# Two stacked graph-attention layers on one core: SyncE transfers in written order, other places for layer 0 steps at the seams, other row-sum chains

## The chip, the cores and the metric

The kernel runs on one core of a Trainium2 chip. The time is the device time of one execution in microseconds; of the kernel before there are three runs, with a median of 4371.78 us (4368.92 to 4374.29). Everything else is read from one profiled execution.

## The reference

Eight samples of 2048 nodes with 256 features; one adjacency matrix for all. Two layers, each with a residual and a layer norm:

```python
# layer 0, 8 heads of 32 features
x_proj = einsum('bnd,hdf->bhnf', x, W)
e = leaky_relu(e_src[..., :, None] + e_dst[..., None, :], 0.2) + softplus(beta) * log(adj + 1e-6)
attn = softmax(where(adj > 0, e, -inf), axis=-1)
x1 = layernorm(x + (attn @ x_proj) @ W_out.T)
# layer 1, one head of 256
e = leaky_relu((x1 @ W1) @ (x1 @ W2).T, 0.2)
attn = softmax(where(adj > 0, e, -1e12), axis=-1)
out = layernorm(x1 + relu(attn @ (x1 @ W3)))
```

## The kernel before

Node tiles have 128 rows, so a sample has 16. All arithmetic is in float32.

**Layer 0** (class `Gat`) of one sample takes 64 steps, called units here: four passes `hp` of two heads, each over 16 key tiles `jt`. A unit loads one row block of the transposed mask m^T (`mt`, 128x2048, 1 MB; line 200, two buffers), lets VectorE form the unnormalised attention of each head over all 2048 queries in one instruction (`s`, line 342, from the query factors `c`, the key factors `re` and `mt`; four buffers, so two units), and lets TensorE add its product with the projected values `v` into `val` and with the key factors into the row sums `den` (both line 367). For some key tiles, listed in `SUMMED` (line 67), `den` is left out: a chain of tiles is added up in `d`, the first tile by ScalarE (line 355), the others by VectorE (line 349, issued one unit later), and one product with ones at the end of the pass puts the chain into `den`. At the end of a pass `finish` (line 371) copies `val` into `ht` and `den` into `dn`, spreads the four rows of `dn` over the partitions (`rc`, line 385), takes the reciprocal (386), stores it (387), and after every second pass loads it broadcast (`rb`, 393) and multiplies `ht` (395).

**Between the layers**, `output` (line 397) forms x1 in four groups of four tiles: product y with W_out (420), residual, layer norm, store. `turn` (line 436) transposes x1 and forms h3 = x1 W3, two tiles at a time.

**Layer 1** (class `Dot`) takes 16 steps, one for each query tile. A step transposes the first quarter of the weights p of its tile (line 500), forms the scores e of the next tile (481), adds the mask `pen` and takes the minimum of the negative on VectorE (486), exponentiates on ScalarE (487), transposes the rest and accumulates p h3 in `acc` (516). Then it scales, loads its x1 row (521), adds it (524), normalises and stores.

**Order.** TensorE's order is the written one (`manual_schedule`, line 86). Everything else, SyncE's transfers among it, is ordered by the framework's planner, which takes the instructions by their place in the program and by when it expects them ready. Every engine works through its own list in order; SyncE issues all loads and most stores and waits at a transfer until its buffer is free.

The program first builds m^T, runs layer 0 of sample 0 and projects all other samples; v and the factors `re` of samples 2 to 7 are stored in DRAM. Then the main loop (line 595) works on layer 1 of sample b-1 and layer 0 of sample b together: `layer_0(n)` places n units, and `dot.step` takes a function that is called at three places of a step: ahead of it, after the next tile's scores (before the accumulation), and after the accumulation. At the hand-over, the seam, steps 14 and 15 of the sample before are still to be done; then come the x1 groups, `turn`, and the first query tile of the next sample. Units 0 and 1 follow step 14's accumulation, then come step 15, two x1 groups, units 2 and 3, two groups, units 4 and 5, and units 6 to 11 between the pieces of `turn`. `fresh.load()` (line 603) loads v, for which there is one buffer, and `re`, for which there are three. The tag `ht` of `chunk` has three buffers, shared by `dn`, the x groups and the query projections h1.

## Time and profile before

| | before |
|---|---|
| median of 3 runs | 4371.78 us |
| profiled execution | 4370.06 us, its span 4368.3 us |
| granted TensorE clock | 0.989 |
| TensorE busy | 4226.0 us, 97% |
| VectorE busy | 3618.2 us, 83% |
| ScalarE busy | 1669.7 us, 38% |
| m^T loads | 496 of 1024 KB, 4.9 us to landing |
| period of one sample (2 to 7) | 506 us |

The span is the time from the first to the last instruction of the profiled execution. In a group of instructions, the line reads: line of the code, engine, operation, output<-inputs, shapes and count | busy time in us, mean ns of one | idle time of the engine just before them, and what ended it. In an engine's list in order of time, the first number is the start in us, the second the length of the stretch; a bracket gives the idle time before it and what ended it. Matmuls overlap, so TensorE's lengths overlap as well.

### The profile page before, as it was taken

How to read it: one execution, taken by the hardware profiler on the slowest of the kernel's cores; microseconds unless marked ns; L12 is line 12 of the kernel's file. 1: busy time of each engine (PE TensorE's matmuls, PEld its weight loads, DVE VectorE, ACT ScalarE, POOL GpSimd, SP SyncE). 2: the span in 40 equal slices, each digit the busy share in tenths (PEclk: the TensorE clock that was granted, in tenths of full speed). 3: DMA queues.
4: the chain of work that ended last, by engine and by line, in shares of the span. 5: the costliest groups of instructions: out<-in, count | busy, mean ns of one | idle time of the engine just before them, and what ended most of it. 6: DMA issues, size and time to landing. Idle time of an engine off the chain costs nothing.

```text
span 4368.3 us, 59747 instructions
## 1 busy us (share of the span) xinstructions
PE 4226.0 (97%) x25008; PEld 2221.4 (51%) x25008; DVE 3618.2 (83%) x2598; ACT 1669.7 (38%) x3021; POOL 9.5 (0%) x14
## 2 busy tenths in 40 slices
PE   7999899999999999999999999999999999999999
PEld 4444344455455554445545554455455554555666
DVE  6888888998889898998889988898999988898222
ACT  6522233333333433333333334333333333333454
POOL 0000000000000000000000000000000000000000
PEclk9999899999999999999999999999999999999999
DMA  8877666656555654556555565555545565554211
GB/s 252 297 267 281 230 214 215 228 195 226 186 189 189 215 194 156 201 185 220 178 193 193 177 212 183 190 193 208 184 171 193 193 221 179 188 184 141 72 50 41
DMA packets 250959, 839.10 MB, mean 192 GB/s; under 512 B 32320, under 2 KB 150848, under 8 KB 175424
## 3 DMA queue, kind: packets, MB, share of 16 engines
q1 hardware_dynamic: 215360, 801.71, 52.6%
q10 hardware_dynamic: 35328, 33.56, 2.2%
q8 instruction: 196, 3.21, 0.3%
q14 instruction: 75, 0.61, 0.0%
HBM read 761.53 MB, written 73.14 MB: 191 GB/s over the span
## 4 chain that ended last, share of the span: by engine, by line
PE 64%; DVE 16%; issue 7%; DMA 2%; ACT 2%; SPq 0%; ACTq 0%; DVEq 0%; POOLq 0%
PE acc L516 18%; PE e L481 16%; PE val L367 13%; DVE s L342 10%; PE den L367 9%; PE pt L500 5%; DVE d L349 4%; DMA mt<-mt_d 2%; PE h1p L471 1%; PE y L420 1%; PE proj L268 1%; DVE st L424 1%; DVE ht L422 1%; PE h3p L451 1%; DVE p L486 0%
## 5 line engine op out<-in xcount | busy, mean ns | idle before, releaser
L342 DVE SCALAR_TENSOR_TENSOR s<-c,re,mt 128x2048 f32<-128x2048 f32 x1024 | 2351.1, 2342 | 179.2 <-PE den L367 113.8
L367 PE MATMUL val<-s,v 128*32 128x512 f32 x8192 | 1031.4, 604 | 69.3 <-DVE s L342 69.2
L516 PE MATMUL acc<-h,pts 128*128 128x256 f32 x4096 | 951.0, 380 | 4.3 <-ACT pts L502 4.0
L481 PE MATMUL e<-x1t,h 128*128 128x512 f32 x2048 | 906.3, 595 | 6.5 <-ACT h L473 6.5
L516 PEld LDWEIGHTS acc<-h,pts 128*128 128x128 f32 x4096 | 749.3, 190 | 94.5 <-ACT pts L502 8.3
L367 PE MATMUL den<-s,re 128*32 128x512 f32 x5568 | 702.2, 596 | 3.2 <-ACT dn L382 3.2
L349 DVE SCALAR_TENSOR_TENSOR d<-s,re,d 128x2048 f32<-128x2048 f32 x272 | 631.4, 2343 | 0.1
L481 PEld LDWEIGHTS e<-x1t,h 128*128 128x128 f32 x2048 | 379.1, 190 | 459.4 <-issue 416.7
L367 PEld LDWEIGHTS val<-s,v 128*32 128x32 f32 x8192 | 245.9, 110 | 692.7 <-issue 513.9
L502 ACT COPY pts<-pt 128x512 f32<-128x512 f32 x512 | 298.3, 583 | 738.0 <-PE pt L500 731.7
L483 ACT ACTIVATE p<-e 128x512 f32<-128x512 f32 x512 | 302.9, 595 | 433.6 <-PE e L481 430.1
L486 DVE CUSTOM_DVE_ANT_0 p<-p,pen 128x2048 f32<-128x2048 f32 x128 | 292.9, 2289 | 210.9 <-ACT p L483 210.3
L367 PEld LDWEIGHTS den<-s,re 128*32 128x32 f32 x5568 | 193.0, 111 | 426.1 <-issue 412.4
L500 PEld LDWEIGHTS pt<-ident,p 128*128 128x128 f32 x2048 | 240.1, 141 | 227.8 <-issue 156.1
L487 ACT ACTIVATE p<-p,neg 128x2048 f32<-128x2048 f32 x128 | 256.6, 2005 | 224.0 <-DVE neg L486 224.0
L500 PE MATMUL pt<-ident,p 128*128 128x128 f32 x2048 | 318.6, 279 | 14.4 <-ACT p L487 14.4
L524 DVE TENSOR_TENSOR z<-z,x1r 128x256 f32<-128x256 f32 x128 | 53.8, 421 | 178.7 <-ACT z L523 175.3
L523 ACT ACTIVATE z<-acc,rec 128x256 f32<-128x256 f32 x128 | 60.6, 474 | 365.5 <-PE acc L516 332.8
L268 PE MATMUL proj<-wp,xt 128*128 128x272 f32 (+1 forms) x512 | 132.3, 402 | 11.6 <-ACT both L272 8.5
L451 PE MATMUL h3p<-w3s,x1t 128*128 128x256 f32 x512 | 120.8, 381 | 2.6 <-ACT x1t L446 2.6
L355 ACT ACTIVATE d<-s,re 128x2048 f32<-128x2048 f32 x56 | 111.9, 2002 | 23.0 <-DMA xg<-in_x_dram 16.1
L268 PEld LDWEIGHTS proj<-wp,xt 128*128 128x128 f32 x512 | 93.3, 192 | 51.4 <-issue 21.0
(89 smaller groups left out, 1886.0 us busy)
## 6 DMA issues: line engine op xcount, KB each, us to landing
mt<-mt_d SPq DMA_DIRECT2D x496, 1024.0 KB, 4.9
c<-c_d SPq DMA_DIRECT2D x64, 1024.0 KB, 6.3
pen<-pen_d SPq DMA_DIRECT2D x112, 512.0 KB, 3.4
xg<-in_x_dram SPq DMA_DIRECT2D x60, 512.0 KB, 5.7
adj_t<-in_adj_dram SPq DMA_DIRECT2D x16, 1024.0 KB, 8.0
mt_d<-mt SPq DMA_DIRECT2D x16, 1024.0 KB, 5.6
rb<-rec_d SPq DMA_DIRECT2D x64, 256.0 KB, 4.4
x_d<-ht ACTq DMA_DIRECT2D x32, 512.0 KB, 3.9
```

What stands on the lines that cost most here:

```text
L268: nc.tensor.matmul(t[:, 0:cols], xt[:, kc, ts(it % IG, P)], wp[:, kc, 0:cols], start=(kc == 0), stop=(kc == KC - 1))
L342: nc.vector.scalar_tensor_tensor(sa, self.cs[a], self.re[:, 0, jt, h:h + 1], mt, ALU.max, ALU.mult)
L349: nc.vector.scalar_tensor_tensor(d, sa, e[:, jt - 1, h:h + 1], d, ALU.mult, ALU.add)
L367: nc.tensor.matmul(dst[ts(q, DH), ts(c, BK)], weights[q % 2], s[q % 2][:, ds(q // 2 * HALF + c * BK, BK)], start=start, stop=stop)
L451: nc.tensor.matmul(t[:, ts(i, D)], x1t[:, kc, ts(2 * (j - 1) + i, P)], w3s[:, kc, :], start=(kc == 0), stop=(kc == KC - 1))
L481: nc.tensor.matmul(t, self.h1[:, kc, ts(it % IG, P)], self.x1t[:, kc, ts(c, BK)], start=(kc == 0), stop=(kc == KC - 1))
L483: nc.scalar.activation(p[:, ts(c, BK)], t, AF.Prelu, alpha=ALPHA)
L486: nc.vector.tensor_tensor_reduce(p, p, pen, -1.0, FMAX, ALU.add, ALU.min, neg)
L487: nc.scalar.activation(p, p, AF.Exp, bias=neg, scale=-1.0, accum_out=den)
L500: nc.tensor.transpose(t[:, ts(k, P)], p[:, ts(g * IG + k, P)], ident)
L502: nc.scalar.copy(pt, t)
L516: nc.tensor.matmul(acc, now[:, ts(k, P)], self.h3[:, j, :], start=(j == 0), stop=(j == NT - 1))
```

## The change

From the main loop on, SyncE's order is the written one too. m^T loads are placed two units ahead of their use and c loads as soon as a buffer is released in the written order (`load_ahead`, `follow`). `finish` becomes a generator that a pass's next units carry on, one part a unit (`later`): after its copies, the loads of `rc` with the reciprocal are placed two units later, the store one unit after that, and rb one more. rb takes two half tiles from the tag `ht` instead of one whole tile of the chain's tag `d`. pen_d is stored after its first use. The chains have three key tiles (2, 4, 5) in pass 0, and in the others five tiles for sample 1 and seven for samples 2 to 7. At the seam, x1 groups, `turn` and pairs of units alternate, three x groups are loaded ahead, and 20 units are placed before the regular steps, where there were 16.

```diff
@@ -64,7 +64,9 @@
     NP = H // HP
     IG = BK // P
-    SUMMED = [(), (1, 3, 6, 9, 12)] + [(1, 3, 6, 8, 11, 13)] * (B - 2)
+    SUMMED = [[()] * NP, [(2, 4, 5)] + [(1, 4, 7, 10, 13)] * (NP - 1)]
+    SUMMED += [[(2, 4, 5)] + [(1, 3, 5, 7, 9, 11, 13)] * (NP - 1)] * (B - 2)
     const = ctx.enter_context(tc.tile_pool(name="const", bufs=1))
     dram = ctx.enter_context(tc.tile_pool(name="dram", bufs=1, space=DRAM))
@@ -210,7 +212,6 @@
             a = chunk.tile([P, HALF], I32, tag="ht", name="adj_r", bufs=3)
             nc.sync.dma_start(a, adj[ts(it, P), ts(s, HALF)])
             nc.vector.tensor_scalar(pen[:, ts(s, HALF)], a, 0.0, NO_EDGE, ALU.is_le, ALU.mult)
-        nc.sync.dma_start(pen_d[ts(it, P), :], pen)
         return pen
     def layer_norm(z):
@@ -237,6 +238,7 @@
             self.b = b
             self.units = ((hp, jt) for hp in range(NP) for jt in range(NT))
             self.ms, self.mts = [], []
+            self.later = gats[b - 1].later if b > 1 else []
         def begin(self, kept):
@@ -315,6 +317,21 @@
             nc.sync.dma_start(c, c_d[self.b, h:h + 1, :].to_broadcast([P, N]))
             return c
+        def load_ahead(self):
+            self.mt_loads = (load_mt(jt, False) for _ in range(self.b, B) for _ in range(NP) for jt in range(NT))
+            self.c_loads = (gats[b].query_rows(h) for b in range(self.b, B) for h in range(H))
+            self.mts, self.cs_ahead = [], []
+            for _ in range(2):
+                self.cs_ahead.append(next(self.c_loads))
+                self.mts.append(next(self.mt_loads))
+            self.cs_ahead.append(next(self.c_loads))
+        def follow(self, gat):
+            self.mt_loads, self.c_loads, self.mts, self.cs_ahead = gat.mt_loads, gat.c_loads, gat.mts, gat.cs_ahead
         def more_mt(self, count, ahead=0):
             while len(self.mts) < min(count, NT):
@@ -327,23 +344,36 @@
             for _ in range(count):
                 hp, jt = next(self.units)
+                for work in list(self.later):
+                    if next(work, self) is self:
+                        self.later.remove(work)
                 if jt == 0:
-                    self.cs = [self.query_rows(hp * HP + a) for a in range(HP)]
+                    if self.b > 0:
+                        self.cs = [self.cs_ahead.pop(0) for _ in range(HP)]
+                    else:
+                        self.cs = [self.query_rows(hp * HP + a) for a in range(HP)]
                     self.val = pacc.tile([P, HALF], F32, tag="val", name="val")
                     self.den = pacc.tile([P, HALF], F32, tag="den", name="den")
                 first = self.b == 0 and hp == 0
                 if first:
                     self.more_mt(jt + 2, jt > 0)
-                mt = self.mts[jt] if first else load_mt(jt, self.b == 0)
+                if self.b > 0:
+                    mt = self.mts.pop(0)
+                else:
+                    mt = self.mts[jt] if first else load_mt(jt, True)
                 s = []
                 for a in range(HP):
                     h = hp * HP + a
                     sa = wide_tile("s", "s", 4)
                     nc.vector.scalar_tensor_tensor(sa, self.cs[a], self.re[:, 0, jt, h:h + 1], mt, ALU.max, ALU.mult)
                     s.append(sa)
+                    if self.b > 0 and jt == NT - 1:
+                        self.cs_ahead += [c for c in [next(self.c_loads, None)] if c]
+                if self.b > 0:
+                    self.mts += [t for t in [next(self.mt_loads, None)] if t]
                 v, e = self.v, self.re[:, 1]
                 heads = [hp * HP + a for a in range(HP)]
-                chain = SUMMED[self.b]
+                chain = SUMMED[self.b][hp]
                 if jt - 1 in chain[1:]:
                     for d, sa, h in zip(self.sums, self.last, heads):
                         nc.vector.scalar_tensor_tensor(d, sa, e[:, jt - 1, h:h + 1], d, ALU.mult, ALU.add)
@@ -359,7 +389,13 @@
                 if chain and jt == NT - 1:
                     self.products(self.den, [ones] * HP, self.sums, False, True)
                 if jt == NT - 1:
-                    self.finish(hp)
+                    work = self.finish(hp)
+                    next(work)
+                    if self.b == 0:
+                        for _ in work:
+                            pass
+                    else:
+                        self.later.append(work)
         def products(self, dst, weights, s, start, stop):
             for c in range(HALF // BK):
@@ -380,19 +417,24 @@
                                self.val[ts(s, HP * DH), :].rearrange("p (t i) -> p t i", i=P))
             dn = chunk.tile([P, HALF], F32, tag="ht", name="dn", bufs=3)
             nc.scalar.copy(dn, self.den)
+            yield
+            yield
             rc = small.tile([P, HALF // DH], F32, name="rc", bufs=1)
             for q in range(4):
                 nc.sync.dma_start(rc[ts(q, DH), :], dn[q * DH:q * DH + 1, :])
             nc.vector.reciprocal(rc, rc)
+            yield
             nc.sync.dma_start(rec_d[b, hp].rearrange("q (p c) -> (q p) c", c=HALF // DH), rc)
             if lo == 0:
                 return
-            rb = wide_tile("rb", "d", 2)
-            for a in range(2 * HP):
-                src = rec_d[b, hp - 1 + a // HP, a % HP::HP, :]
-                nc.sync.dma_start(rb[ts(a, DH), :].rearrange("p (s i) -> p s i", s=2),
-                                  bass.AP(tensor=src.tensor, offset=src.offset, ap=[[0, DH]] + list(src.ap)))
-            nc.vector.tensor_mul(ht, ht, rb.rearrange("p (t i) -> p t i", i=P))
+            yield
+            for s in range(2):
+                rb = chunk.tile([P, HALF], F32, tag="ht", name="rb", bufs=3)
+                for a in range(2 * HP):
+                    nc.sync.dma_start(rb[ts(a, DH), :], rec_d[b, hp - 1 + a // HP, s * HP + a % HP:s * HP + a % HP + 1, :]
+                                      .to_broadcast([DH, HALF]))
+                half = ht[:, ts(s, NT // 2), :]
+                nc.vector.tensor_mul(half, half, rb.rearrange("p (t i) -> p t i", i=P))
         def output(self):
@@ -405,11 +447,12 @@
                 xs.append(chunk.tile([P, IG, D], F32, tag="ht", name="xg", bufs=3))
                 nc.sync.dma_start(xs[g], xb[:, ts(g, IG), :])
-            load(0)
-            load(1)
+            for g in range(NB - 1):
+                load(g)
+            yield
             for g in range(NB):
-                if g + 2 < NB:
-                    load(g + 2)
+                if g == 2:
+                    load(NB - 1)
                 st = small.tile([P, IG, nc.vector.BN_STATS_DIM], F32, name="st4", bufs=1)
                 mv = small.tile([P, IG, nc.vector.BN_AGGR_DIM], F32, name="mv4", bufs=2)
                 z = self.ht[:, ts(g, IG)].rearrange("p t k i -> p t (k i)")
@@ -484,6 +527,8 @@
             neg = small.tile([P, 1], F32, name="neg")
             den = small.tile([P, 1], F32, name="den1")
             nc.vector.tensor_tensor_reduce(p, p, pen, -1.0, FMAX, ALU.add, ALU.min, neg)
+            if self.b == 0:
+                nc.sync.dma_start(pen_d[ts(it, P), :], pen)
             nc.scalar.activation(p, p, AF.Exp, bias=neg, scale=-1.0, accum_out=den)
             self.ahead = p, den
@@ -591,6 +638,8 @@
                 next(weights, None)
+    ctx.enter_context(tc.manual_schedule(engines={nc.sync.engine}))
     dot = None
     for b in range(1, B + 1):
         gat, fresh = gats[b - 1], gats[b] if b < B else None
@@ -599,38 +648,43 @@
             if fresh:
                 fresh.step(count)
-        if b > 1 and fresh:
+        if b == 1:
+            fresh.load_ahead()
+        elif fresh:
             fresh.load()
-        rows = gat.output()
-        def output(count):
-            for _ in range(count):
-                next(rows)
+            fresh.follow(gat)
+        rows, turns = gat.output(), gat.turn()
         if dot is None:
             layer_0(4)
-            output(2)
+            next(rows)
             next(projections)
-            output(2)
             layer_0(2)
         else:
-            dot.step(lambda k: layer_0((0, 0, 2)[k]))
-            dot.step()
-            for _ in range(2):
-                output(2)
-                layer_0(2)
-        for k, _ in enumerate(gat.turn()):
-            if k % 2 == 1 and k < 7:
+            dot.step(lambda k: layer_0((0, 2, 2)[k]))
+            if not fresh:
+                for work in gat.later:
+                    for _ in work:
+                        pass
+            next(rows)
+            dot.step(lambda k: layer_0((0, 2, 0)[k]))
+        for g in range(NB + 2):
+            if g < NB:
+                next(rows)
+            if g > 1:
+                next(turns)
+                next(turns)
+            if g < NB + 1:
                 layer_0(2)
         dot = Dot(gat)
         dot.step(lambda k: layer_0((2, 0, 2)[k]))
+        count = NP * NT - 20
         for i in range(NT - 3):
-            dot.step(lambda k: layer_0((0, 2 - (i % 3 == 2), 2)[k]))
+            n = (i + 1) * count // (NT - 3) - i * count // (NT - 3)
+            dot.step(lambda k: layer_0((0, n - 2, 2)[k]))
     dot.step()
     dot.step()
```

More of the change, by code (lines that the diff above doesn't have):

```diff
@@ L526, in step @@
             nc.scalar.dma_start(out[self.b, ts(it, P), :], z)
-    gats = [Gat(b) for b in range(B)]
+    gats = []
+    for b in range(B):
+        gats.append(Gat(b))
     g0 = gats[0]
```

## The prediction

> **What bounds the kernel now.** I read the page first, then the busy time by stretch, then the instructions of TensorE, VectorE and SyncE in order of time around one hand-over between samples.
>
> ```profile
> PE 4226.0 (97%) x25008; PEld 2221.4 (51%) x25008; DVE 3618.2 (83%) x2598; ACT 1669.7 (38%) x3021; POOL 9.5 (0%) x14
> ...
> L342 DVE SCALAR_TENSOR_TENSOR s<-c,re,mt 128x2048 f32<-128x2048 f32 x1024 | 2351.1, 2342 | 179.2 <-PE den L367 113.8
> ...
> L349 DVE SCALAR_TENSOR_TENSOR d<-s,re,d 128x2048 f32<-128x2048 f32 x272 | 631.4, 2343 | 0.1
> ```
>
> TensorE is busy 97% of the span, so at most about 140 us can be won. The busy time by stretch, for one sample's period (506.2 us, the same for samples 2 to 7) and for ten-microsecond pieces of its seam (the stretch from query tile 14 of one sample to the first query tile of the next):
>
> ```profile
> 2042.80:2549.00 506.20, 496.70 (x2947) 255.76 (x2946) 449.90 (x316) 186.94 (x325) 0.00 (x0) 0.99 0.55 192
> ...
> 2060.00:2070.00 10.00, 4.45 (x26) 0.70 (x18) 10.00 (x14) 2.58 (x6) 0.00 (x0) 0.84 0.31 107
> 2070.00:2080.00 10.00, 9.49 (x55) 4.81 (x56) 10.00 (x7) 4.24 (x8) 0.00 (x0) 0.81 0.77 259
> ```
>
> The columns are TensorE, weight loads, VectorE, ScalarE and GpSimd busy, then the granted clock. VectorE is full from 2050 to 2130 and TensorE waits; elsewhere TensorE is full. TensorE in order of time shows the hole and what ended it:
>
> ```profile
> 2058.89 1.93 PE L367 MATMUL val<-s,v 128*32 128x512 f32 x16
> 2060.63 1.90 PE L367 MATMUL den<-s,re 128*32 128x512 f32 x16
> 2067.95 1.92 PE L367 MATMUL val<-s,v 128*32 128x512 f32 x2 [5.41 <-DVE s L342]
> 2070.27 2.78 PE L367 MATMUL val<-s,v 128*32 128x512 f32 x11 [0.41 <-DVE s L342]
> ```
>
> From 2009.26 (query tile 14 starts; T0) to 2129 the bracketed waits are 0.29, 5.41, 0.41, 0.24, 0.89 and 0.81: 8.05 us. The clock of 0.84 and 0.81 costs 1.6 + 1.9 = 3.5 us more. That is the loss of one seam, 11.5 us; the other 390 us of a period show about 1.5 us of idle. SyncE and the transfers that matter below:
>
> ```profile
> 2002.78 0.32 SPq L200 DMA_DIRECT2D mt<-mt_d  x1
> 2005.95 0.32 SPq L308 DMA_DIRECT2D v<-v_d  x1
> ...
> 2035.57 0.32 SPq L200 DMA_DIRECT2D mt<-mt_d  x1
> 2035.93 1.45 SPq L310 DMA_DIRECT2D re<-re_d  x1
> ```
>
> The next sample's projections v can only be loaded when TensorE's last product with the old v is done (2005.8). Its score factors re have three buffers and were fetched a whole sample early. Median time to landing: v 8.8 us, re 6.0, m^T 4.9, c 6.3.
>
> **What the Trainium skill says.** "Perfetto Trace Analysis", Optimization Strategy: find the gaps within one regime and what ends them; the averages (97 and 83%) hide this seam. "DMA: Bandwidth & Descriptors", Anatomy of one DMA: a semaphore wait happens on the issuing sequencer, so whatever is written behind a waiting transfer waits too; the trace agrees, SyncE waits 1791.8 us for scores before m^T loads. Same page, Queues, rings and completion order: SyncE owns one row of rings, consumed in order; the trace fits, a 128 KB x1 row on SyncE lands in 4.8 us behind m^T loads, a 128 KB output on ScalarE's queue in 1.7. "TensorE: Matmul & The Clock Gate", Part 1: an idle window of about 3.4 us lowers the clock; the trace agrees after the 5.41 us.
>
> **Prices** from the seam's rows. TensorE: first transpose 0.5, e 6.86, the rest of a query tile 8.3 (2016.62 to 2024.94), a unit 3.46, a unit whose row sum is left to a chain 1.73, one x1 group 3.5. VectorE back to back: the two scores of a unit 4.53 (four instructions in 9.14), a chained tile 4.53, p 2.3, an x1 group 3.5 (its four lines are 15.1 a period, less overlap), a query tile's end 0.95. The score tiles have four buffers, so scores of unit k start only when unit k-2 is consumed by TensorE, and by the chain if k-2 is chained.
>
> **The change part by part.**
> 1. *SyncE in written order, m^T two steps ahead.* m^T keeps two buffers, so a load still starts when the scores two units back are done. VectorE waits only 37.9 us for m^T and 9.1 for c in the whole run, mostly off the path: gain at most a few us, taken as 0. But it pins everything else. `load` stands at the head of a seam: v waits for TensorE until 2005.8, and re, which came a sample early, now follows v in the queue. v lands at T0+5.5; re about 1.1 later (as it followed one m^T load of 4.9 in 6.0): T0+6.6. Behind them wait pen of tile 15 and m^T of unit 2. Before, units 0 and 1 were scored from 2004.23 to 2013.4.
> 2. *Units moved forward.* Units 0 and 1 now stand right behind e of tile 15, at T0+7.35 instead of T0+15.7; 2 and 3 after tile 14, 4 and 5 inside tile 15; then pairs between x1 groups. 20 units instead of 16 before the steady steps, 44 instead of 48 in them.
> 3. *Chains.* Samples 2 to 7: 3+7+7+7 = 24 tiles as with 4x6, so no TensorE or VectorE work in sum. Sample 1: 18 for 20, two more row sums of 1.73 = +3.5 us TensorE, and -9 VectorE, which is not the bound there on average. In pass 0, tiles 4 and 5 follow each other.
> 4. *Row-sum reciprocals later, rb in two halves.* rc issues when unit 0 is scored (T0+11), lands in 2.5, reciprocal at T0+18, store 2.8, rb after the scores of unit 2 (T0+22.5), eight issues of 0.66 (3 took 1.98), landing 4.4: T0+32, two multiplications 2.4. y starts after T0+40: hidden by some 6 us; otherwise y is late by what is missing. The third x load waits for these halves' buffers, with m^T of unit 6 behind it, needed at T0+45: covered.
> 5. *pen_d store* after p: no other SyncE instruction lies between, 0. x1 rows are loaded behind the last m^T of a step, not early: they land about when the accumulation ends, 0; without that cover part of 4.8 us of VectorE per query tile.
>
> **The seam, summed.** Without waits TensorE would run: e to T0+7.35, u0 10.8, u1 14.3, acc 22.6, u2 (chained) 24.3, u3 27.8, transpose 28.3, u4, u5 (chained) 31.7, acc 40.0, y0 43.5, u6, u7 50.4, y1 53.9, u8 57.4, u9 starts at 57.4.
> VectorE: s0 from 6.6 to 11.1; p of tile 15 and s1 by 17.9. So u1 ends at 19 to 21.4 (5 to 7 late), u2 at 29 to 31.4. s4 can start only then; with the multiplications and a row end near it, it is done at T0+36 (33.7 to 38). From there VectorE has s5, chain 4, s6, chain 5 (18.1), the x1 group and a row end (4.5), s7 (4.5): u7 starts at 63.1, due at 47.0. Then s8, s9 and group 1 (12.6): u9 starts at 75.7 against 57.4: 18.3 us of waiting. Afterwards TensorE has x1^T and h3 between the pairs and leads. Against 8.05 this is +10.2 a seam; bounds: +3.0 if re cost nothing (s4 done at 28.8), +12.3 with s4 at 38. I take +10 because the v and re order follows from the code; the clock loss is taken as equal (0 to +3.5). Six seams: 60.
>
> The first seam (sample 1, no load): six units instead of four stand before y, VectorE-bound already (waits of 6.01, 3.75, 1.70 and 1.35 there). By the same count u7 ends near 537 with y1 to y3 (10.5) open, where before was at 538 with u6, u7 (6.9) open: +4, and 2 at u9, less 1: +5 (3 to 10). The last seam has no layer 0: 0.
>
> Steady steps: by rows, a step inside a pass has VectorE 25.6 of TensorE's 26.1 us now (38 instructions in 13 units, 3.38 units), before 26.35 of 27.4: tighter, but covered; 0, up to 30 in all if the cover is gone. Sum: 60 + 5 + 3.5 = 68.5 on the profiled execution's 4370.1 (span 4368.3 and 1.8 around it), 4438.6; the median of the runs is 1.7 above that execution: 4440.
>
> **Rivals.**
> *The seam closes.* Between 2013 and 2041 VectorE idles 14.5 us (2.26, 1.47, 2.34, 1.01, 4.27, 2.40, 0.80); the early units use it, the waits shrink to about 4 us and the clock stays up: -7.5 x 6 - 5, about 4320. It decides if s4 and both chain tiles come so early that u9 waits under 8 us in sum, s4 done before T0+26. Against: u2's own place ends at 24.3, which puts s4 at 28.8 at best.
> *The stall only moves:* s4 near 28.8 and no loss of clock[...]: +3 - 3.5 a seam, about 4370.
> *Steady steps give as well:* late x1 rows hold VectorE in its fixed order, and at each pass's end two 1 MB c loads stand before m^T, landing it some 3 us later. 5 to 10 us a period more: about 4490. For: VectorE at 98% inside a pass. Against: it often waits for TensorE there.
>
> **How the numbers follow.** Forecast 0.58, steady loss 0.22, stall moves 0.08, seam closes 0.12. The forecast's own range is 4391 (all low bounds) to 4475. For 8 in 10 I take 4362 to 4505: the seam closing falls below, part of the steady loss above. A measurement of this kernel tells about 0.2% (9 us) from no change; so faster 0.12, same 0.08, slower 0.80.
>
> **What would show it.** After: period of a sample near 516; SyncE issuing re right behind v at each seam; first scores of a sample starting 10 us after v is issued, with VectorE waiting for re; TensorE waiting for scores at units 0, 1, 5 and 7, 15 us or more between tile 14 and the first query tile; y with no wait for rb. Wrong if re lands before T0, if u7 follows u6 closely, or if the period's other 390 us change by more than 3.

## The result and the profile after

The changed kernel takes 4508.73 us (median of four runs, 4504.14 to 4512.47), the kernel before 4370.82 on the same chip: a ratio of 1.0314 [1.0296, 1.0332]. It is 138 us slower: forecast was 4440, some 70 us slower, with 4505 as the upper end. The profiled execution has a span of 4502.4 us against 4368.3, so +134.1, and these lie here:

| part of the span | before | after | difference |
|---|---|---|---|
| up to the first load of v (`v<-v_d`; it ends sample 1) | 988.6 | 1019.3 | +30.7 |
| one period, mean of five from load of v to load of v (before: 511.0 once, then 506.0 to 506.3) | 507.1 | 523.7 | +16.6 |
| six periods | | | +101.2 |
| from the last query tile 14 on | | | +2.2 |

The page of the changed kernel, the lines that answer to those of before, and one more (busy time, mean ns, idle time just before and what ended most of it):

```profile
PE 4279.3 (95%) x25040; PEld 2217.8 (49%) x25040; DVE 3604.1 (80%) x2610; ACT 1661.5 (37%) x3021; POOL 9.5 (0%) x14
...
L368 DVE SCALAR_TENSOR_TENSOR s<-c,re,mt 128x2048 f32<-128x2048 f32 x1024 | 2362.7, 2341 | 300.6 <-PE den L403 161.7
L379 DVE SCALAR_TENSOR_TENSOR d<-s,re,d 128x2048 f32<-128x2048 f32 x268 | 622.8, 2342 | 0.0
...
L569 DVE TENSOR_TENSOR z<-z,x1r 128x256 f32<-128x256 f32 x128 | 53.8, 420 | 205.9 <-ACT z L568 97.8
```

VectorE does no more than before (3604.1 us), and idles more in front of the scores, 300.6 us against 179.2. TensorE's busy time grew by 53 us, though its work grew by 3.5. Part of that is the clock, as the busy times by stretch show (TensorE, weight loads, VectorE, ScalarE, GpSimd, granted clock, share and rate of the DMA engines). First one whole period, then pieces of its seam:

```profile
2066.27:2590.23 523.96, 504.23 (x2948) 254.88 (x2944) 448.91 (x316) 185.87 (x324) 0.00 (x0) 0.98 0.52 185
2070.00:2080.00 10.00, 7.11 (x19) 2.93 (x17) 2.38 (x4) 5.29 (x12) 0.00 (x0) 1.00 0.83 339
2080.00:2090.00 10.00, 6.39 (x26) 1.36 (x30) 10.00 (x7) 2.09 (x2) 0.00 (x0) 0.54 0.32 107
2110.00:2120.00 10.00, 2.86 (x17) 0.60 (x16) 10.00 (x8) 0.61 (x2) 0.00 (x0) 0.75 0.32 105
2120.00:2130.00 10.00, 9.32 (x43) 4.70 (x42) 10.00 (x7) 2.50 (x7) 0.00 (x0) 0.74 0.64 238
```

Read in pieces of ten microseconds over the whole period, TensorE's idle time is 19.7 us (before 9.5), and the clock loss, each piece times one less its clock, is 10.2 us (before 3.4). The two overlap, because TensorE is idle for a part of the time at half clock. Of this period's 20.5 us at half clock it was busy for 12.5 (before 5.4 of 6.8), so the clock lengthened its work by 6.3 us (before 2.7). Counted without overlap, +10.2 us of idle time and +3.6 of clock make 13.8 of this period's +18.0; the other 4.2 are busy time at full clock, and no run here shows where they come from. Over the whole run the clock's part of the 53 us is 22. TensorE in order of time at the same seam; query tile 14 starts at 2069.59 (T0):

```profile
2081.05 1.91 PE L403 MATMUL val<-s,v 128*32 128x512 f32 x2 [3.94 <-DVE s L368]
2085.53 2.78 PE L403 MATMUL val<-s,v 128*32 128x512 f32 x11 [2.56 <-DVE s L368]
...
2119.36 1.92 PE L403 MATMUL val<-s,v 128*32 128x512 f32 x2 [7.14 <-DVE s L368]
2121.96 3.48 PE L403 MATMUL val<-s,v 128*32 128x512 f32 x14 [0.68 <-DVE s L368]
...
2133.66 3.62 PE L463 MATMUL y<-wot,ht 128*128 128x256 f32 x16
```

Two holes: 6.50 us at unit 0 and 7.82 at unit 5. SyncE shows what is ahead of the first one, and VectorE both:

```profile
2065.12 0.43 SPq L566 DMA_DIRECT2D x1r<-x_d  x1
2066.27 0.32 SPq L310 DMA_DIRECT2D v<-v_d  x1
2066.64 0.58 SPq L312 DMA_DIRECT2D re<-re_d  x1
2067.26 0.44 SPq L209 DMA_DIRECT2D pen<-pen_d  x1
2085.50 0.32 SPq L202 DMA_DIRECT2D mt<-mt_d  x1
```

```profile
2073.20 0.42 DVE L569 TENSOR_TENSOR z<-z,x1r 128x256 f32<-128x256 f32 x1 [8.81 <-DMA x1r<-x_d]
...
2078.65 2.35 DVE L368 SCALAR_TENSOR_TENSOR s<-c,re,mt 128x2048 f32<-128x2048 f32 x1 [4.35 <-DMA re<-re_d]
...
2110.17 1.22 DVE L437 TENSOR_TENSOR ht<-ht,rb 128x1024 f32<-128x1024 f32 x1
2111.31 4.61 DVE L379 SCALAR_TENSOR_TENSOR d<-s,re,d 128x2048 f32<-128x2048 f32 x2
2115.83 1.22 DVE L437 TENSOR_TENSOR ht<-ht,rb 128x1024 f32<-128x1024 f32 x1
2116.97 2.34 DVE L368 SCALAR_TENSOR_TENSOR s<-c,re,mt 128x2048 f32<-128x2048 f32 x1
```

VectorE waits 8.81 us for the x1 row of tile 13, which stands on SyncE behind two loads of c and one of m^T, then 4.35 us for re. The scores of unit 5 start at 2116.97, behind both halves of the rb multiplication and chain tile 4.

### The profile page after: what moved, and what is told of

It is laid out like the page before. It is cut to its first block, busy times and chain, and to the rows that moved or that the text cites. A ratio compares the mean times of both kernels' runs of the same rounds, so it can differ in the third digit from the quotient of the medians.

```text
span 4502.4 us, 59957 instructions
## 1 busy us (share of the span) xinstructions
PE 4279.3 (95%) x25040; PEld 2217.8 (49%) x25040; DVE 3604.1 (80%) x2610; ACT 1661.5 (37%) x3021; POOL 9.5 (0%) x14
## 4 chain that ended last, share of the span: by engine, by line
PE 49%; DVE 23%; issue 11%; DMA 6%; ACT 3%; SPq 0%; DVEq 0%; POOL 0%; ACTq 0%; POOLq 0%
DVE s L368 14%; PE acc L561 13%; PE e L524 11%; PE val L403 11%; PE den L403 6%; DVE d L379 4%; PE pt L545 3%; DMA mt<-mt_d 3%; DVE p L529 3%; PE h3p L494 2%; DMA re<-re_d 1%; PE h1p L514 1%; ACT p L532 1%; PE y L463 1%; DMA adj_r<-in_adj_dram 1%
## 5 line engine op out<-in xcount | busy, mean ns | idle before, releaser
L368 DVE SCALAR_TENSOR_TENSOR s<-c,re,mt 128x2048 f32<-128x2048 f32 x1024 | 2362.7, 2341 | 300.6 <-PE den L403 161.7
L403 PE MATMUL val<-s,v 128*32 128x512 f32 x8192 | 1069.2, 611 | 136.4 <-DVE s L368 136.2
L561 PEld LDWEIGHTS acc<-h,pts 128*128 128x128 f32 x4096 | 748.7, 191 | 117.2 <-ACT pts L547 30.7
L270 PE MATMUL proj<-wp,xt 128*128 128x272 f32 (+1 forms) x512 | 134.1, 404 | 15.0 <-ACT both L274 11.1
L494 PE MATMUL h3p<-w3s,x1t 128*128 128x256 f32 x512 | 125.0, 388 | 14.9 <-ACT x1t L489 13.9
```

What stands on the lines that cost most here:

```text
L270: nc.tensor.matmul(t[:, 0:cols], xt[:, kc, ts(it % IG, P)], wp[:, kc, 0:cols], start=(kc == 0), stop=(kc == KC - 1))
L368: nc.vector.scalar_tensor_tensor(sa, self.cs[a], self.re[:, 0, jt, h:h + 1], mt, ALU.max, ALU.mult)
L403: nc.tensor.matmul(dst[ts(q, DH), ts(c, BK)], weights[q % 2], s[q % 2][:, ds(q // 2 * HALF + c * BK, BK)], start=start, stop=stop)
L494: nc.tensor.matmul(t[:, ts(i, D)], x1t[:, kc, ts(2 * (j - 1) + i, P)], w3s[:, kc, :], start=(kc == 0), stop=(kc == KC - 1))
L561: nc.tensor.matmul(acc, now[:, ts(k, P)], self.h3[:, j, :], start=(j == 0), stop=(j == NT - 1))
```

## The experiments

Theory after the result: the written order delays re, and with that VectorE's start into a seam in which VectorE is full; the early chain tiles (2, 4, 5) sit in the same stretch; something else, not foreseen, lengthens sample 1. Rivals: the chains or the unit order alone are the loss; or the pinned SyncE order costs in the steady steps.

One measure is used throughout, and it is read from one period of each profile. A seam is taken from the scores e of tile 15 to the e of the next sample's first query tile, the steady part from there to the next seam. The changed unit order puts four more units into the seam, and chains move row sums about; so each value stands against the time of before (106.0 and 400.0 us) corrected by that content: 3.46 a unit, 1.73 less where the row sum is left to a chain, 1.9 for the chain's product with ones. For the changed kernel that is 106.0 + 4 x 3.46 + 1.9 + 2 x 1.73 = 125.3 for a measured 140.3, so +15.0. Single periods differ by steps of the clock. The mean of the five seams and steady parts lies within 1 us of the table, but for the seams of e1 (+5.5), e11 (+0.9), e13 (+5.1) and e16 (+0.2), and the steady part of e12 (+7.2). The last column holds idle time and clock loss as first defined, with their overlap.

| run | us | ratio to before, interval | first load of v | mean period | seam | steady | TensorE idle, clock loss in one period |
|---|---|---|---|---|---|---|---|
| before | 4370.8 | | 988.6 | 507.1 | 0 | 0 | 9.5, 3.4 |
| after | 4508.7 | 1.0314 [1.0296, 1.0332] | 1019.3 | 523.7 | +15.0 | +3.0 | 19.7, 10.2 |
| e1 re early | 4459.3 | 1.0198 [1.0183, 1.0213] | 1027.4 | 515.2 | +4.3 | +3.0 | 13.7, 5.2 |
| e2 planned SyncE | 4430.8 | 1.0132 [1.0117, 1.0147] | 1018.0 | 511.8 | +5.4 | +0.5 | 12.5, 5.1 |
| e3 late chain | 4492.1 | 1.0275 [1.0260, 1.0291] | 1022.2 | 520.9 | +13.3 | +2.9 | 17.7, 6.8 |
| e5 old unit order | 4425.9 | 1.0121 [1.0104, 1.0138] | 1007.7 | 512.6 | +3.7 | +2.3 | 11.9, 3.4 |
| e4 before, new chains | 4429.6 | 1.0128 [1.0113, 1.0143] | 987.6 | 517.2 | +1.6 | +8.5 | 13.9, 5.1 |
| e9 rb as before in sample 0 | 4496.1 | 1.0280 [1.0265, 1.0296] | 1012.5 | 523.4 | +14.5 | +3.0 | 19.4, 10.3 |
| e10 = e1 + late chain + rb | 4425.8 | 1.0123 [1.0108, 1.0138] | 1011.7 | 511.9 | +1.3 | +2.9 | 11.5, 0 |
| e12 before, late chain | 4349.3 | 0.9939 [0.9923, 0.9956] | 986.0 | 504.5 | -9.9 | +8.5 | 7.8, 1.7 |
| e7 = e1 + old unit order, old chains | 4372.4 | 0.9999 [0.9991, 1.0008] | 1017.4 | 502.9 | -4.2 | 0.0 | 7.4, 0 |
| e11 = e2 + late chain + rb | 4374.8 | 1.0007 [0.9999, 1.0016] | 988.0 | 507.9 | +4.1 | +0.4 | 11.3, 1.7 |
| e13 = e1 + x1 rows early | 4434.5 | 1.0143 [1.0128, 1.0158] | 1019.0 | 512.2 | +2.6 | +1.1 | 12.3, 3.5 |
| e14 before, other chains | 4318.2 | 0.9877 [0.9862, 0.9892] | 980.5 | 500.2 | -9.9 | +2.7 | 5.0, 0 |
| e15 = e1 + old chains | 4485.3 | 1.0256 [1.0241, 1.0271] | 1024.9 | 520.0 | +11.8 | +1.9 | 17.7, 5.1 |
| e16 = e1 + old unit order | 4403.5 | 1.0068 [1.0053, 1.0083] | 1009.4 | 509.6 | +1.5 | +2.3 | 10.4, 5.2 |
| e17 = e7 + rb as before | 4359.5 | 0.9968 [0.9955, 0.9981] | 1004.1 | 502.2 | -4.2 | -0.4 | 7.0, 0 |
| e18 = e17 + chains of e14 | 4297.6 | 0.9824 [0.9808, 0.9841] | 986.2 | 495.5 | -12.3 | +0.6 | 2.8, 0 |

### One part of the change undone

**e1, re one sample ahead.** The load of re is taken out of `load` and put at the head of the sample before:

```diff
@@ class Gat
             nc.sync.dma_start(self.v, v_d[self.b])
+        def load_re(self):
             self.re = small.tile([P, 2, NT, H], F32, name="re", bufs=3)
             nc.sync.dma_start(self.re, re_d[self.b])
@@ main loop
+        if b + 1 < B:
+            gats[b + 1].load_re()
         rows, turns = gat.output(), gat.turn()
```

> The changed kernel with the score factors re of the next sample loaded one sample ahead, so that only v is loaded at the head of a seam. Seam theory (re behind v makes units 0 and 1 late, 6.5 us of waiting and the clock after it): that wait goes, the later wait at unit 5 stays, about 10 us less for each of six seams, near 4450 us. Rival, SyncE's written order costs everywhere (rows of x1, m^T behind others), not by re: less than 15 us gained, 4495 or more. Rival, the chain tiles 4 and 5 set the seam and re only moves the wait along: 4490 to 4509, with the wait at unit 5 longer.

49.5 us faster. TensorE at its seam (T0 at 2063.3):

```profile
2071.83 1.92 PE L405 MATMUL val<-s,v 128*32 128x512 f32 x16 [0.98 <-DMA v<-v_d]
...
2102.96 1.92 PE L405 MATMUL val<-s,v 128*32 128x512 f32 x2 [7.14 <-DVE s L370]
```

The 6.50 us at unit 0 became 0.98 us of waiting for v; the wait at unit 5 is the same to a hundredth. So the late re costs 10.7 us in this seam (9.6 on the mean of five), and not the hole at unit 5. The clock loss falls from 10.2 to 5.2.

**e2, SyncE ordered by the planner again.**

```diff
-    ctx.enter_context(tc.manual_schedule(engines={nc.sync.engine}))
```

> The changed kernel with SyncE's transfers ordered by the planner again (the line that sets the written order is taken out); seam order and chains as changed. Seam theory: re comes early again and m^T no longer waits behind the reciprocals at the first seam (15 us), but the chain tiles 4 and 5 still hold VectorE in the seam: near 4430. Rival, the written order of SyncE is the whole cause: 4370 or less. Rival, the written order is not a cause: 4490 to 4509.

77.9 us faster, some 12 us a period: the number came as expected, but not all of its reason. The first load of v stays at 1018.0, and TensorE still waits 14.75 us for the scores of sample 1's unit 2, a wait that was expected to go with the written order. So what lengthens sample 1 is not the written order alone, and that the sum came right is in part luck. The steady part falls to +0.5.

**e3, pass 0's chain late.**

```diff
-    SUMMED = [[()] * NP, [(2, 4, 5)] + [(1, 4, 7, 10, 13)] * (NP - 1)]
-    SUMMED += [[(2, 4, 5)] + ...
+    SUMMED = [[()] * NP, [(7, 10, 13)] + [(1, 4, 7, 10, 13)] * (NP - 1)]
+    SUMMED += [[(7, 10, 13)] + ...
```

> The changed kernel with the chain of pass 0 at key tiles 7, 10, 13 instead of 2, 4, 5; same count. Seam theory: VectorE has two chained tiles less (9 us) between units 4 and 9, so the wait of 7 to 8 us at unit 5 and the clock after it go: about 10 us less a seam, near 4450, units 0 and 1 still waiting. Rival, re alone sets the seam: no more than 10 us gained. Rival, chains elsewhere (7 tiles in passes 1 to 3) are the cause: no change or slower.

A miss: only 16.7 us. The wait at unit 5 shrank to 1.55, but the one at unit 0 stayed (4.61 and 2.56), and waits of 0.86 to 1.45 came at units 4, 9 and 15. Tiles 7 and 10 still lie in the stretch where VectorE is full; that they are the reason is not shown.

**e5, the unit order of before at the seam and in the steady steps.** SyncE's written order, the late re and the new chains stay; the late reciprocals are all placed ahead of the x1 groups:

```diff
-            dot.step(lambda k: layer_0((0, 2, 2)[k]))
+            dot.step(lambda k: layer_0((0, 0, 2)[k]))
...
-            dot.step(lambda k: layer_0((0, 2, 0)[k]))
+            dot.step()
+            for _ in range(2):
+                for _ in range(2):
+                    next(rows)
+                layer_0(2)
```

> The changed kernel with the order of work at the seams and in the steady steps as before the change (units 0 and 1 after tile 14, x1 groups by twos, 16 units ahead of the steady steps); SyncE's written order, the chains and the late reciprocals stay, the latter placed ahead of the x1 groups. Seam theory: unit 0 stands 8 us later, so re is there in time, and the period returns to 506 to 510 us: near 4395, with the first seam's m^T wait still there. Rival, the written order of SyncE costs wherever it stands: 4470 or more.

82.8 us faster, but 31 us short of the 4395 expected and not back at before: a period of 512.6 rather than 507.

### What the chains cost by themselves

**e4, the kernel before with the changed chains alone** (the new `SUMMED`, and `chain = SUMMED[self.b][hp]`).

> The kernel before with only the change's row-sum chains (three tiles 2, 4, 5 in pass 0; five or seven tiles in the other passes). Theory: the steady part's +3.6 us a period comes from passes of seven chained tiles, in which a query tile has less TensorE work (two chained tiles in each three or four units) for the same VectorE work, and the seam's share comes from where units stand: then the period rises by 3 to 5 us and the time is 4390 to 4405. Rival: the chains alone cost nothing (24 chained tiles a sample in both), and what the steady part lost comes from the written order and the late x1 rows: period within 1 us of 507, 4368 to 4380 (sample 1 has 3.5 us more of TensorE).

57.7 us slower, more than either expected. Of 10.1 us a period the seam has 1.6; 8.5 are in the steady part. Waits of 2.79 us for scores and 1.15 for h appear in the passes with seven chained tiles, where before showed 0.48 to 0.93.

**e12, the kernel before with `(10, 12, 14)` in pass 0** and else the chains of e4.

> The kernel before, but pass 0 sums only key tiles 10, 12, 14 in a chain and the other passes seven tiles (five in sample 1). Theory: VectorE is what limits the seam; six chained tiles of pass 0 cost it 27 us there, and with the chain late that work leaves the seam, its wait of 5.41 us and the clock loss go: period 507 to about 499 to 501, 4325 to 4340. Rival: what leaves the seam tightens the passes with seven chained tiles, where VectorE is at 98 per cent: period 505 to 508, 4360 to 4385.

22.6 us faster than before, between theory and rival, and both hold at once: the seam is 9.9 us shorter, and the steady part, with its passes of seven, gives back 7.2 on the mean (8.5 in the period of the table).

**e14, one of the sevens back to six.**

```diff
-    SUMMED = [(), (1, 3, 6, 9, 12)] + [(1, 3, 6, 8, 11, 13)] * (B - 2)
+    SUMMED = [[()] * NP, [(10, 12, 14)] + [(1, 4, 7, 10, 13)] * (NP - 1)]
+    SUMMED += [[(8, 10, 12, 14), (1, 3, 5, 7, 9, 11, 13), (1, 3, 6, 8, 11, 13), (1, 3, 5, 7, 9, 11, 13)]] * (B - 2)
```

> The kernel before with other chains only: pass 0 tiles 8, 10, 12, 14, passes 1 and 3 seven tiles, pass 2 six (24 in sum, as before); sample 1 has 10, 12, 14 and then five. Against the run with 10, 12, 14 and seven in passes 1 to 3 (4349): if the wait of 2.79 us in pass 2 comes from its seventh tile, it goes with its clock loss, and tile 8 costs nothing at the seam's end: 4322 to 4335. Rival: tile 8 falls into the seam and brings VectorE's wait back: 4350 to 4370.

4318.2, somewhat better than expected: the wait of 2.79 and the clock loss are gone, the steady part is +2.7, and the seam keeps its 9.9. What the chain does depends on where its tiles fall, not on their number: in samples 2 to 7 there are 24 in before, e4, e12 and e14.

### The longer first part

In the changed kernel TensorE waits 15.20 us for the scores of sample 1's unit 2. That wait, then VectorE and SyncE ahead of it:

```profile
514.74 1.92 PE L403 MATMUL val<-s,v 128*32 128x512 f32 x2 [15.20 <-DVE s L368]
```

```profile
512.33 9.14 DVE L368 SCALAR_TENSOR_TENSOR s<-c,re,mt 128x2048 f32<-128x2048 f32 x4 [7.99 <-DMA mt<-mt_d]
```

```profile
497.54 2.70 SPq L434 DMA_DIRECT2D rb<-rec_d  x6
502.14 0.34 SPq L297 DMA_DIRECT2D v_d<-v  x1
502.52 0.43 SPq L298 DMA_DIRECT2D re_d<-re  x1
503.00 18.82 SPq L202 DMA_DIRECT2D mt<-mt_d  x4
```

The m^T loads stand behind the rb loads and behind two stores that wait for VectorE (of the reciprocals, 3.0 us, and of v, 1.8). **e9** leaves everything changed but forms rb of sample 0 as before:

```diff
+            if b == 0:
+                rb = wide_tile("rb", "d", 2)
+                for a in range(2 * HP):
...
+                nc.vector.tensor_mul(ht, ht, rb.rearrange("p (t i) -> p t i", i=P))
+                return
             yield
             for s in range(2):
                 rb = chunk.tile([P, HALF], F32, tag="ht", name="rb", bufs=3)
```

> The changed kernel, but the row-sum factors rb of sample 0 are formed as before (one whole tile in the buffers of d, four loads, one multiplication); samples 1 to 7 as changed. Theory: the halves of rb in the three buffers ht, with eight loads, hold SyncE's queue in sample 0, so that m^T of sample 1's unit 2 comes late and TensorE waits 15 us there: that wait goes, the first loads of v come at about 1000 rather than 1019, and the time falls by 15 to 25 us to about 4488. Rival: what delays m^T is the order of the loads in front of it (rc, rb, v, re of the last projections), which stays: the 15 us wait stays and the time is 4503 to 4510.

SyncE of e9 at the same place issues two m^T loads before the store of v, and TensorE waits 5.16 us for unit 2:

```profile
486.79 0.53 SPq L202 DMA_DIRECT2D mt<-mt_d  x1
...
492.44 0.42 SPq L202 DMA_DIRECT2D mt<-mt_d  x1
493.02 0.82 SPq L434 DMA_DIRECT2D rb<-rec_d  x2
496.57 0.34 SPq L297 DMA_DIRECT2D v_d<-v  x1
```

The mechanism is right, its size is half: 12.6 us less, first load of v at 1012.5, not 1000. The planner does not remove it. With the halves TensorE's wait at this place is 14.8 to 17.9 us in all runs; the shortest is e2, without the written order:

```profile
520.62 1.92 PE L403 MATMUL val<-s,v 128*32 128x512 f32 x2 [14.75 <-DVE s L368]
```

With rb of sample 0 as before it is 4.0 to 6.0 us under the planner (before, e4, e11, e12, e14) and 5.2 to 10.6 in the written order (e9, e10, e17, e18).

**e10** is e1, e3's chain and e9's rb together; **e11** is e2 with the same two.

> The changed kernel with re loaded one sample ahead, pass 0's chain on tiles 7, 10, 13, and rb of sample 0 as before. If the three causes add: 4459 (re ahead alone) less 17 (chain late alone) less 20 (rb of sample 0): about 4420, period 512. If the late chain was worth little only because VectorE started the seam late behind re, it now gives its full 7 us a seam: about 4397, period 508. If rb of sample 0 does nothing: 20 us more in either case, with the first load of v at about 1025.

> The changed kernel without the written order of SyncE (the planner places the transfers), pass 0's chain on tiles 7, 10, 13, and rb of sample 0 as before: what is left is the new order of units at the seam, rb in halves from sample 1 on, and chains of seven. Theory: with the early chain out of the seam its VectorE wait goes as it went in the kernel before (12.7 us a period between the two places of the chain): 4431 less 13 (rb) less 40 to 70: 4350 to 4380, period 501 to 505. Rival: the chain's place is worth only the 3 us a period it was worth in the written order: 4395 to 4405.

e10 gave 4425.8 and a period of 511.9: about the sum of the three single gains (4430). e11 gave 4374.8, in the theory's range, but the period is 507.9, not 501 to 505; the larger gain is in the first part, 1018.0 to 988.0.

### What is left of the written order

**e7** has re ahead, and the unit order and the chains of before (e1, e5 and the old `SUMMED`): left are SyncE's written order with m^T two units ahead, the late x1 rows, and rc and rb later and in halves. **e17** has rb of sample 0 as before in addition (e9).

> The changed kernel with re loaded one sample ahead, the seam in the order of before and the chains of before: what is left of the change is SyncE's written order with m^T two ahead, the late x1 rows, and rb in halves with eight loads. Theory: these cost only what was seen ahead of the first load of v (about 20 us with the old seam) and next to nothing a period: period 507 to 509, 4388 to 4402. Rival: the late x1 rows and the pinned m^T order are the steady loss: period 511 or more, 4412 or more.

> The run that has only the written order left (re ahead, unit order and chains of before; 4372), with rb of sample 0 as before. Theory: rb in halves holds SyncE in front of sample 1's m^T: its 15 us wait goes, first load of v from 1017 to 990 to 1003, 4345 to 4360. Rival: other loads of the written order hold it and rb gives only the 12 us it gave in the changed kernel or less: 4360 to 4372, first v 1005 to 1017.

e7 is equal to before (0.9999), but by two unequal parts: 28.8 us longer to the first load of v, and periods 4.2 us shorter, better than theory and rival. One period of e7, busy times and clock:

```profile
2027.16:2528.98 501.82, 494.42 (x2948) 254.93 (x2944) 449.07 (x317) 186.26 (x324) 0.00 (x0) 1.00 0.55 194
```

The clock is full, the wait of 5.41 gone. In the kernel before VectorE stood idle for 4.27 and 2.40 us ahead of the first x1 group, and had tile 3 of pass 0, the first that it adds to the chain, done 55.6 us after T0, behind two groups. In e17, whose seam measures the same 101.8 us as e7's, that tile is done 35.4 us after T0, ahead of the first group's residual (T0 is at 2009.26 and 2014.82):

```profile
2058.87 2.32 DVE L349 SCALAR_TENSOR_TENSOR d<-s,re,d 128x2048 f32<-128x2048 f32 x1
...
2062.59 2.32 DVE L349 SCALAR_TENSOR_TENSOR d<-s,re,d 128x2048 f32<-128x2048 f32 x1
```

```profile
2044.44 2.35 DVE L380 SCALAR_TENSOR_TENSOR d<-s,re,d 128x2048 f32<-128x2048 f32 x1
...
2047.84 2.35 DVE L380 SCALAR_TENSOR_TENSOR d<-s,re,d 128x2048 f32<-128x2048 f32 x1
```

Which of the parts left brings the 4.2 us was not tried one by one.

e17 gives 12.9 us, about what e9 gave. Its time of 4359.5 lies at the edge between theory and rival and its v at 1004.1 between them; the size of the gain is the rival's. Against before, 15.5 us remain up to the first load of v: 7.3 of them come before layer 1's first scores e (586.9 for 579.6), and 8.3 in the steps of sample 1 after that. What lengthens those steps was not tried.

**e13, x1 rows at the start of their step.** e1, and:

```diff
@@ Dot.step
             self.at += 1
+            xr = row_tile("x1r")
+            nc.sync.dma_start(xr, x1_d[self.b, ts(it, P), :])
             fill(0)
...
-            xr = row_tile("x1r")
-            nc.sync.dma_start(xr, x1_d[self.b, ts(it, P), :])
```

> The changed kernel with re loaded one sample ahead and each x1 row loaded at the start of its query tile's step instead of its end. Against re ahead alone (4459). Theory: the late x1 rows hold VectorE in the steady part (42.5 us of waits there) and this is the loss of 3.5 us a period outside the seam: 15 to 25 us less, 4434 to 4444. Rival: VectorE has room outside the seam, and the waits only move to the next thing it waits for: 4455 to 4463.

24.8 us less than e1, the upper end of what the theory said, but only half of it where the theory put it: 1.9 us a period in the steady part (2.3 on the mean of five), and the first load of v 8.4 us earlier. The seam gains 1.7 in the period of the table, but 0.4 on the mean.

### Unit order and chains, crossed

**e15** is e1 with the chains of before, **e16** is e1 with the unit order of before (and the late reciprocals placed as in e5); with e1 and e7 they make a square.

> The changed kernel with re loaded one sample ahead and the chains of before (1, 3, 6, 8, 11, 13 in every pass); the seam's new unit order stays. Theory: the early adjacent chain tiles are the loss (58 us when added alone to the kernel before): 4459 less 45 to 60: 4399 to 4414, period 504 to 506. Rival: the unit order itself is the loss, since six chain tiles of pass 0 still fall into the seam with more units in it: 4440 to 4460, period 512 to 515.

> The changed kernel with re loaded one sample ahead and the unit order of before at the seam; the new chains stay. With re late this gave 4426. Theory: the late re costs some 8 us a period wherever the units stand, because VectorE starts the seam late behind it: 4370 to 4385, period 504 to 506. Rival: in the old unit order the scores wait for nothing at that place, so re early gains at most 2 us a period, and the chains cost the 10 us a period that they cost when added alone: 4413 to 4430.

| re ahead, written order | chains of before | changed chains |
|---|---|---|
| unit order of before | 4372.4 (seam -4.2) | 4403.5 (+1.5) |
| changed unit order | 4485.3 (seam +11.8) | 4459.3 (+4.3) |

For e15 the rival is right, and more than right: the unit order alone costs 113 us. In the changed order the changed chains help by 26 us, in the old one they cost 31; neither "the chains" nor "the order" has a price by itself. One period of e15 and its TensorE in the first half of the seam:

```profile
2067.73:2587.51 519.78, 502.10 (x2948) 254.80 (x2944) 450.36 (x317) 186.99 (x324) 0.00 (x0) 0.99 0.52 187
```

```profile
2102.59 2.78 PE L404 MATMUL val<-s,v 128*32 128x512 f32 x11 [2.35 <-DVE s L369]
...
2137.52 1.04 PE L404 MATMUL val<-s,v 128*32 128x512 f32 x2 [2.69 <-DVE s L369]
2139.85 2.78 PE L404 MATMUL val<-s,v 128*32 128x512 f32 x11 [1.28 <-DVE s L369]
```

Most waits of e15's seam are for scores, 11.6 of 13.9 us. By the prices, the four units that were moved in cost VectorE 4 x 4.53 = 18.1 us of scores and one chained tile 4.53, together 22.6; TensorE 14.0. Where VectorE is already full the difference of 8.6 us should be lost; this is an estimate. Measured, TensorE's idle time in the period grows by 10.3 us from e7 to e15 and its clock loss by 5.1, against 16.0 us between the two seams. The changed chains take three of six chained tiles out of pass 0, which fits that they help here.

e16 fell between theory and rival. Against e5 (4425.9) re ahead is worth 22.4 us in the old unit order, not 49.5. Its largest wait for scores sits behind adjacent chain tiles 4 and 5:

```profile
2089.46 2.32 DVE L381 SCALAR_TENSOR_TENSOR d<-s,re,d 128x2048 f32<-128x2048 f32 x1
2091.77 2.35 DVE L381 SCALAR_TENSOR_TENSOR d<-s,re,d 128x2048 f32<-128x2048 f32 x1
2094.03 4.61 DVE L370 SCALAR_TENSOR_TENSOR s<-c,re,mt 128x2048 f32<-128x2048 f32 x2
2098.55 4.61 DVE L381 SCALAR_TENSOR_TENSOR d<-s,re,d 128x2048 f32<-128x2048 f32 x2
```

Nine of the fourteen microseconds are chain work; TensorE waits 3.15 us at 2105.48.

**e18** is e17 with the chains of e14.

> The previous one with the chains 8, 10, 12, 14 in pass 0 and seven, six, seven after it, which gave 4318 when put alone into the kernel before. Theory: the written order and the late chain relieve the same wait at the seam, so they do not add: period 498 to 501, and the first part stays some 10 to 20 us longer: 4318 to 4340. Rival: they add: period 495 or 496, 4290 to 4310.

The rival was right: they add. The periods of e17 and e14, 4.9 and 6.9 us shorter than before, would make 495.3, and it is 495.5. With 4297.6 us, 1.76% below before (0.9824 [0.9808, 0.9841]), it is the fastest of all. One period:

```profile
1977.59:2471.92 494.33, 491.56 (x2948) 254.66 (x2944) 447.98 (x317) 185.75 (x324) 0.00 (x0) 1.00 0.55 197
```

TensorE idles 2.8 us in it.

## Why the prediction was right and wrong

**What bounds the seam: right.** VectorE limits it, TensorE the rest. e12 and e14, which take chain work out of the seam, show it by 9.9 us a seam each, e18 against e17 by 8.1.

**v and re: right in mechanism, short in size.** v was issued at T0 - 3.3, as forecast, re right behind. v took 12.1 us (median) where 8.8 was taken, and re was there at T0 + 9.1, not 6.6. The first scores came 12.4 us after v was issued, not 10. e1 prices it at 49.5 us. The Trainium skill, "DMA: Bandwidth & Descriptors", Anatomy of one DMA, places a transfer's semaphore wait on the issuing sequencer. The trace agrees: re had a free buffer, and was issued 0.37 us behind v, which waited for TensorE.

**The waits of one seam: right in sum, partly in the wrong place.** 17.0 us from T0 to the first query tile against 18.3 forecast. But u7, forecast to be 16 us late, follows u6 closely, which the prediction had named as a sign against itself. The step "s5, chain 4, s6, chain 5" missed that both rb multiplications and chain 4 go ahead of both scores of unit 5. The hole came two units earlier, at unit 5, ahead of the accumulation and the first x1 group, which gave VectorE the time it needed for units 6 and 7. y waited for no rb: right.

**The clock loss "taken as equal": failed.** By the prediction's own measure it rose from 3.4 to 10.2 us in the period, and by 34.5 us from the first load of v to the end of the run. The forecast had waits at four units, one of some 16 us, in place of the one of 5.41, and did not go on from there to more lost clock; 3.5 a seam was its upper bound. Without what falls on waits already counted, the clock cost 3.6 us more a period, which is at that bound. So of the 8 us by which this period's +18.0 goes beyond the forecast's 10, some 3.6 are clock; 4.2 are the busy time at full clock that stays open.

**Steady steps 0: failed.** They lost 3.0 us a period. The step that failed is "tighter, but covered": its sum does not follow from its own prices. By these a query tile takes 0.5 + 6.86 + 8.3 = 15.7 us of TensorE, and 3.38 units, seven in thirteen of them chained, 8.5 more. That is 24.2 us a step, not 26.1, and before the change 25.5, not 27.4. Against VectorE's 25.6 and 26.35 nothing is covered inside a pass, less so after the change. "x1 rows 0" failed too: VectorE waits 8.81 us for one at the head of the seam, and e13 brings back 1.9 us of the steady loss by loading them early. But late rows are not enough: e7 has them too, with the unit order and the chains of before, and its steady part is 0.0 (+0.7 on the mean). With the changed chains it is +2.3 (e16), with the changed unit order +1.9 (e15). So the rival "steady steps give as well", whose 4490 was the nearest of the four times, is half shown; that the two c loads before m^T have a share was not tried.

**The first seam +5 (3 to 10): failed, the largest miss in one place.** Up to the first load of v it is +30.7, where the prediction had 5 and the 3.5 of sample 1's chains; 9.4 of it lie ahead of sample 1, where the prediction saw nothing change. The step that failed: forming rb in halves was costed for the seams of samples 2 to 7 alone, where x1 hides it. In sample 0 its loads put m^T late, under the planner too (e2), and the wait at unit 2 goes from 4.0 to 10.6 us without the halves to 14.8 to 17.9 with them. The written order costs as well, in part later, in the steps of sample 1. The first load of v comes at 988.0 with both rb as before and the planner (e11), 1018.0 with halves and the planner (e2; its chain differs too), 1004.1 with rb as before and the written order (e17; 1012.5 with the changed unit order, e9), and 1017.4 with both (e7). Either alone does half or more of it.

**Chains "no work in sum", so only +3.5: failed as a step.** The sum is the same, the places are not. In the unit order of before, seven chained tiles in a pass cost 7.2 to 8.5 us a period under the planner (e12, e4) and 2.3 in the written order (e16); in the changed unit order, under the planner, the steady part is only +0.5 (e2). Why was not tried.

**The seam closes: not here, but the reason for it was sound.** The 14.5 us of VectorE's idle time before the first x1 group can be used: in e7, with the old unit order and re ahead, VectorE is idle for 10.0 us of the seam instead of 15.6, and the seam is 4.2 us shorter.

Summed as the prediction summed: 15.0 + 3.0 us in the period shown instead of 10, mean 16.9 over six, 101 instead of 60; first part 31 instead of 8.5; last seam 2 instead of 0; 134 instead of 68.5.

## What to carry to other kernels

When an engine's order is pinned, walk through its list and ask of each transfer what it waits for and what is late behind it; do it for every phase of the program, also for the one that the change does not aim at. Price a moved unit on each engine at the place where it goes: here four units a sample, moved to where VectorE is full, cost 113 us over the run with the chains of before (e15 against e7). Two edits that draw on the same engine in the same stretch have no prices of their own, so cross them; here one of them changes its sign. And when idle time and lost clock are added up, take out the part that is both.

## What was not expected of the hardware

The clock loss of the periods shown comes in steps: 1.7, 3.4 to 3.5, 5.1 to 5.2, 6.8 and 10.2 to 10.3 us in these runs, multiples of about 1.7, and 0 in five of them. The Trainium skill, "TensorE: Matmul & The Clock Gate", Part 1, describes half clock until a busy window of about 3.4 us has passed; half of 3.4 us is this step, so the runs agree: but for the one at the end of the program, every stretch of half clock in these profiles lasts 3.413 us or a multiple of it, and in each profile all of them start on one grid of 3.413 us. Its idle window of about the same length, taken as a wait of 3.4 us, is no threshold here: in e12 a wait of 2.79 us for the scores of unit 43 comes in six periods, and three of them lose one step. Two pieces of eight microseconds around that wait, equally busy, with clocks of 0.79 and 1.00:

```profile
1337.00:1345.00 8.00, 5.21 (x23) 2.33 (x22) 8.00 (x6) 2.68 (x3) 0.00 (x0) 0.79 0.58 196
1841.00:1849.00 8.00, 5.21 (x31) 2.69 (x30) 8.00 (x6) 2.69 (x3) 0.00 (x0) 1.00 0.55 196
```

What differs is where the wait falls on the grid. In the three periods that lose a step 2.2 to 2.6 us of it lie between two grid points, in the other three at most 1.7. This is one wait in one run; other waits near 2 us went either way. Large holes cost more: in the period shown the changed kernel's 6.5 and 7.8 us come with three steps each, while e10 idles 11.5 us in waits of at most 1.55 and loses no clock there (3.4 and 1.7 us in two of its other periods).
